# Causal attention on one core: the weighing of values moved from the pause between rounds into the round, and the diagonal's maxima split and taken one round later

## The chip, the cores and the metric

The kernel runs on one core of a Trainium2 chip. The metric is the device time of one execution in microseconds (us). A core has five engines that matter here: PE (TensorE, matrix products, with PEld for its weight loads), DVE (VectorE), ACT (ScalarE), POOL (GpSimd) and SP (SyncE, which issues DMAs). Each engine [...]waits for the others by semaphores. Products land in PSUM, which has 8 banks of 512 fp32 columns by 128 partitions.

## The reference

Four sequences of 1024 tokens with 128 features pass four residual blocks: an attention with relative positions, a mixture-of-experts FFN, a causal attention with one shared key and value head, and the same FFN again. The change touches the third block alone:

```python
def _L0_attn_b_ref(x, Wq, bq, Wk, bk, Wv, bv, Wo, bo):
    NUM_HEADS = 16; HEAD_DIM = D_MODEL // NUM_HEADS          # 8
    q = (x @ Wq + bq).reshape(b, t, NUM_HEADS, HEAD_DIM)
    k = x @ Wk + bk                                         # one head for all
    v = x @ Wv + bv
    scores = einsum('bthd,bsd->bhts', q, k) / sqrt(HEAD_DIM)
    scores = scores * mask - 1e10 * (1 - mask)              # causal
    probs = softmax(scores, axis=-1)
    out = einsum('bhts,bsd->bthd', probs, v).reshape(b, t, 128)
    return out @ Wo + bo
x = x + _L0_attn_b_ref(_layernorm(x), ...)
```

## The kernel before

All four blocks are one program. The first attention takes the first 1600 us or so, the FFN f follows (overlapped with the preparation of the causal attention, `b_prep`, line 912), the causal attention runs from about 1800 to 2585 us, and the FFN g ends the program. All of it is written by hand in one order (`tc.manual_schedule()`, line 1165): what the Python calls emit first stands first in each engine's queue.

**The tiles.** A tile n is 128 queries (block i of sequence b). There are 32; `tiles` (line 949) orders them so that each sequence begins while the one before it ends. Heads lie as 4 row groups g (of 32 partitions, 8 of them used and a ninth for the maximum) by 4 positions k, so one product with K = 32 rows of the array serves one group.

**Scores** (`b_scores`, line 959) are computed twice. The first time, with the queries as weights, is only for the maxima: a step is one PSUM bank of `s_b`. The first four steps of a tile are the diagonal block; ACT copies them to `dg` (L980), POOL masks `dg` after the fourth (L988). Steps of the earlier keys are reduced by DVE to `m2` straight from PSUM (L982). In the tile's last step DVE reduces all of `dg` (L993), and a small reduce (L997) writes the negated maxima of all chunks into `mpad`. `found` then holds the tile.

**Queries** (`b_queries`, line 1003): PE turns `mpad` (`mt`, L1008), and DVE adds it to the queries (`qm`, L1010), so that the second product has the maximum subtracted already.

**Weights** (`b_weights`, line 1016): for each key block j, the diagonal first, four products `t_b` (L1027), one for each row group, with the keys as weights and 512 columns (4 positions x 128 queries). ACT exponentiates each into `pt` (L1030). A diagonal `pt` is masked by POOL (L1034). After the fourth group the block is appended to `waiting`.

**Weighing** (`b_weigh`, line 1041): four products `o_b` (L1048), all 128 rows by 32 columns of the array, accumulate one key block into a PSUM bank of a pool of two (`small`). After the tile's last block ACT copies the sum to `oT` (L1055), and a generator `b_out` (line 1058) is put on `going`. Its steps are: nothing, then `tp` (four transposes, L1065, with DVE's `oinv` and `on`), then `y` (one transpose, ACT copies `onT`), then `z` (one product, DVE adds to x). Each call advances it by one.

Every fp32 product appears as two records on PE. `s_b`, `t_b`, `mt`, `tp`, `y`, `z` and the preparation take their banks from one pool of six (`one`, line 733), in which a bank comes free when its reader has read it.

**The rounds** (`causal_attention`, line 1084). There are 576 `t_b` products, 8 to a round, so 72 rounds. Score steps are spread before them: the loop at L1088 finds how many must be done by each round (a tile's scores two rounds ahead of its weights), and CAP limits a round to 10. In round r the loop L1118 to L1122 emits, for q = 0 to 7, one or two score steps and one weight step. Behind the eight comes what I call the pause (L1127 to L1143): the weighing of all waiting blocks but the last two, so of the two blocks that the round before produced; `mt` and `qm` of tiles that were found one round ago (`lag`); one step of each output generator; steps of `b_prep` for the next sequence; and steps of the FFNs (`left_over`, `sending`).

Of the kernel before, what the change touches and what calls it, by code (L numbers as in the profile page):

```python
# [12 lines left out]
F32 = mybir.dt.float32  # L13
I32 = mybir.dt.int32
AF = mybir.ActivationFunctionType
ALU = mybir.AluOpType
AX = mybir.AxisListType

P = 128
# [11 lines left out]
NH = 16  # L31
HD = 8
# [32 lines left out]
def block_kernel(ctx: ExitStack, tc: tile.TileContext, a: dict, out: bass.AP):  # L65
    nc = tc.nc
# [682 lines left out]
    chunks = [(b, c, min(4, TILES - c)) for b in range(B) for c in range(0, TILES, 4)]  # L749
# [199 lines left out]
    tiles = sorted(((b, i) for b in range(B) for i in range(NB)), key=lambda t: (t[1] + 4 * t[0], t))  # L949


    ROUND = 8
    first_round, count = [], 0
    for b, i in tiles:
# [4 lines left out]
    def b_scores(n):  # L959


        b, i = tiles[n]
        qa, ka, _ = prepared[b]
        tok = slice(i * P, (i + 1) * P)
        m2 = fp.tile([P, NH, 3], F32, tag="m2", name=f"m2_{n}")
        dg = fp.tile([P, NH, P], F32, tag="wide", name=f"dg_{n}", bufs=6)
        chunks = [(i * P, P)] + [(c, min(512, i * P - c)) for c in range(0, i * P, 512)]
        steps = []
        for c, (k0, w) in enumerate(chunks):
            nh = min(4, 512 // w)  # L970
            steps += [(c, k0, w, k, nh, g) for k in range(0, 4, nh) for g in range(4)]
        for at, (c, k0, w, k, nh, g) in enumerate(steps):
            ps = one(f"s_b{n}_{at}")
            for q in range(nh):
                nc.tensor.matmul(  # L975
                    ps[:, q * w : (q + 1) * w], qa[rows[g], k + q, tok],
                    ka[rows[g], k0 : k0 + w], start=True, stop=True,
                )
            if c == 0:
                nc.scalar.copy(dg[:, 4 * g : 4 * (g + 1), :].rearrange("p k c -> p (k c)"), ps)  # L980
            else:
                nc.vector.tensor_reduce(  # L982
                    m2[:, 4 * g + k : 4 * g + k + nh, c],
                    ps[:, : nh * w].rearrange("p (k c) -> p k c", c=w), AX.X, ALU.max,
                )
            if at == 3:

                nc.gpsimd.affine_select(  # L988
                    out=dg, in_=dg, pattern=[[0, NH], [-1, P]], compare_op=ALU.is_ge,
                    fill=NEG, base=0, channel_multiplier=1,  # L990
                )
            if at == len(steps) - 1:
                nc.vector.tensor_reduce(m2[:, :, 0], dg, AX.X, ALU.max)  # L993
                mpad = mpads[n % 4]
                mview = mpad.rearrange("p k (g r) -> p g k r", g=4)[:, :, :, HD]
                mv4 = m2.rearrange("p (g k) c -> p g k c", g=4)
                nc.vector.tensor_reduce(  # L997
                    mview, mv4[:, :, :, : len(chunks)], AX.X, ALU.max, negate=True
                )
                found.append(n)  # L1000
            yield

    def b_queries(n):

        b, i = tiles[n]
        mt = one(f"mt_{n}")
        for k in range(4):
            nc.tensor.transpose(mt[:, k * P : (k + 1) * P], mpads[n % 4][:, k, :], ident)  # L1008
        qm = fp.tile([P, 4, P], F32, tag="qm", name=f"qm_{n}", bufs=4)
        nc.vector.tensor_tensor(  # L1010
            qm, prepared[b][0][:, :, i * P : (i + 1) * P],
            mt.rearrange("p (k c) -> p k c", k=4), ALU.add,
        )
        queries[n] = qm

    def b_weights(n):

# [23 lines left out]
    def b_weigh(n, j, pt):  # L1041
        b, i = tiles[n]
        va = prepared[b][2]
        if n not in sums:
            sums[n] = small(f"o_b{n}")
        op = sums[n]
        for g in range(4):
            nc.tensor.matmul(  # L1048
                op[g * 32 : (g + 1) * 32, :], va[:, j, :], pt[:, g, :],
                start=(j == i), stop=(i == 0 or j == i - 1),  # L1050
            )
        if i == 0 or j == i - 1:

            oT = fp.tile([P, 4, P], F32, tag="oT", name=f"oT_{n}", bufs=4)
            nc.scalar.copy(oT.rearrange("p k c -> p (k c)"), sums.pop(n))  # L1055
            going.append(b_out(n, oT))

    def b_out(n, oT):

        b, i = tiles[n]  # L1060
        x_t = xs[b][:, i, :]
        yield
        tp = one(f"tp_b{n}")
        for k in range(4):
            nc.tensor.transpose(tp[:, k * P : (k + 1) * P], oT[:, k, :], ident)  # L1065
        o4 = tp.rearrange("p (k g w) -> p g k w", k=4, g=4)
        oinv = fp.tile([P, 4, 4, 1], F32, tag="oinv", name=f"oinv_{n}")
        nc.vector.reciprocal(oinv, o4[:, :, :, HD : HD + 1])
        on = fp.tile([P, 4, 4, HD], F32, tag="on", name=f"on_{n}", bufs=4)
        nc.vector.tensor_tensor(  # L1070
            on, o4[:, :, :, :HD], oinv.to_broadcast([P, 4, 4, HD]), ALU.mult
        )
        yield
        yp = one(f"y_b{n}")
        nc.tensor.transpose(yp[:, :P], on.rearrange("p g k w -> p (g k w)"), ident)
        onT = fp.tile([P, P], F32, tag="onT", name=f"onT_{n}", bufs=4)
        nc.scalar.copy(onT, yp[:, :P])
        yield
        zp = one(f"z_b{n}")
        nc.tensor.matmul(zp[:, :D], onT, bwo, start=True, stop=True)  # L1080
        nc.vector.tensor_tensor(x_t, x_t, zp[:, :D], ALU.add)
        finished.append(n)

    def causal_attention(left):

        steps_of = [sum(4 * (4 // min(4, 512 // w)) for w in chunk_widths(i)) for b, i in tiles]
        must = []
        for r in range(-2, ROUNDS):  # L1088
            must.append(sum(x for x, f in zip(steps_of, first_round) if f <= r + 2))

        CAP = 10
        cum = list(must)
        for r in range(len(cum) - 2, -1, -1):
            cum[r] = max(cum[r], cum[r + 1] - CAP)
        scores = (None for n in range(len(tiles)) for _ in b_scores(n))
        weights = (None for n in range(len(tiles)) for _ in b_weights(n))

        start = {b: next(r for r, c in enumerate(cum) if c > sum(steps_of[: tiles.index((b, 0))]))
                 for b in range(2, B)}
        coming = {b: b_prep(b) for b in range(2, B)}  # L1100
        second = next(r for r, c in enumerate(cum) if c > sum(steps_of[: tiles.index((1, 0))]))
        taken = 0
        lag = []
        sending, sent, left_over = [], 0, list(left)
        for k, r in enumerate(range(-2, ROUNDS + 4)):
            for b in coming:
                if k == start[b]:
                    for _ in coming[b]:
                        pass
            if k == second:  # L1110
                while 1 not in prepared:
                    left_over = [g for g in left_over if next(g, 0) is None]
            upto = cum[min(k, len(cum) - 1)]
            mine = upto - taken
            taken = upto
            if 0 <= r < ROUNDS:
                given = 0
                for q in range(ROUND):  # L1118
                    while given * ROUND < mine * (q + 1):
                        next(scores)  # L1120
                        given += 1
                    next(weights)  # L1122
            else:
                for _ in range(mine):
                    next(scores)

            now, waiting[:] = waiting[:-2] if r < ROUNDS - 1 else waiting[:], waiting[-2:] if r < ROUNDS - 1 else []  # L1127
            for w in now:
                b_weigh(*w)
            ready, lag = lag, list(found)  # L1130
            found.clear()
            for n in ready:
                b_queries(n)
            going[:] = [g for g in going if next(g, going) is not going]
            for b in coming:
                for _ in range({9: 2, 8: 1, 7: 4}.get(start[b] - k, int(0 < start[b] - k < 7))):
                    next(coming[b], None)
            left_over = [g for g in left_over if next(g, 0) is None]

            if sent < B - 1 and tiles.index((sent, NB - 1)) in finished:  # L1140
                sending.append(sends("g", sent, (1, 3)))
                sent += 1
            sending = [g for g in sending if next(g, 0) is None]  # L1143
        return sending, list(range(sent, B))

    def chunk_widths(i):
# [10 lines left out]
    mpads = []  # L1157
# [3 lines left out]
        mpads.append(mpad)  # L1161

    prepared, queries, sums, found, waiting, going, finished = {}, {}, {}, [], [], [], []

    with tc.manual_schedule():
        left = ffn("f", {
# [74 lines left out]
```

## Time and profile before

| what | us |
|---|---|
| median of three runs (lowest to highest) | 2808.8 (2784.7 to 2812.8) |
| the profiled execution, its own time | 2796.1 |
| its span, first to last instruction | 2794.4 |
| DVE, ACT busy from 1832.2 to 2580.0 (747.8 us) | 431.8, 445.8 |
| t_b products L1027: records, one | 1152, 0.59 at least |
| s_b products L975: records, one | 2304, 0.27 to 0.59 by width |
| o_b products L1048: records, one | 1152, 0.59 |
| exp L1030, one | 0.60 |
| score maxima L982, one | 0.54 to 0.70 |
| POOL's masks L988 and L1034, one | 2.01 |
| qm L1010, one | 0.69 |

How to read it: a record's busy time on PE runs from its start to a modelled end, and records overlap, so that a busy PE can still be made faster if more of its products run at once. PEld is the weight load of a product; its idle time and the releaser of it show what PE's queue waits for. A releaser called "issue" means that the profile shows nothing that was waited for. In the view of waits a line gives the waiting engine and line, the releaser, and then the total in us, the number of times and the longest. The granted clock is TensorE's, 1.00 being full speed.

### The profile page before, as it was taken

The numbers are of one execution on the slowest core, as the hardware profiler recorded it, in microseconds if no ns is written. First come the engines' busy times: TensorE is split into PE (matmuls) and PEld (weight loads), VectorE is DVE, ScalarE is ACT, GpSimd is POOL, SyncE is SP. The second block draws the span as 40 slices with busy tenths as digits, with TensorE's granted clock in tenths as the row PEclk, the third lists the DMA queues.
The fourth block names the chain that finished last, engine by engine and source line by source line (L and its number), as shares of the span: only waits on it lengthen the run. The fifth ranks groups of instructions, "written<-read, shape, count | busy, mean of one in ns | idle before, by whom it ended". The sixth has DMA issues, their size and how long they took to land.

```text
span 2794.4 us, 47349 instructions
## 1 busy us (share of the span) xinstructions
PE 2700.6 (97%) x18928; PEld 1665.0 (60%) x18928; DVE 1406.5 (50%) x3278; ACT 1333.8 (48%) x2478; POOL 540.3 (19%) x693
## 2 busy tenths in 40 slices
PE   6999999999999999999999999999999999999895
PEld 3465666666565656565666676666456456554663
DVE  2335454545545454535454545466546456574444
ACT  2444454443444443534444344555656656556442
POOL 3111000000200001200002006542212215122365
PEclk9999999999999999999999999889989889999897
DMA  8577565664757565657566413200000001000243
GB/s 217 186 245 227 185 199 194 215 200 161 233 169 233 174 204 170 228 173 233 197 213 217 152 49 108 71 14 3 1 1 1 1 1 31 1 7 11 63 119 99
DMA packets 148491, 363.59 MB, mean 130 GB/s; under 512 B 16160, under 2 KB 71872, under 8 KB 147952
## 3 DMA queue, kind: packets, MB, share of 16 engines
q1 hardware_dynamic: 130128, 316.78, 34.9%
q0 software_dynamic: 15552, 40.97, 5.6%
q10 hardware_dynamic: 2592, 2.82, 0.4%
q8 instruction: 150, 2.46, 0.4%
q14 instruction: 69, 0.57, 0.1%
HBM read 176.69 MB, written 183.76 MB: 129 GB/s over the span
## 4 chain that ended last, share of the span: by engine, by line
PE 92%; DVE 2%; issue 2%; DMA 1%; POOL 1%; ACT 1%; another core or an unknown queue 0%; POOLq 0%; ACTq 0%; DVEq 0%
PE op L616 16%; PE rp L555 16%; PE sp L583 15%; PE s_b L975 10%; PE t_b L1027 9%; PE o_b L1048 5%; PE h_f L790 3%; PE h_g L790 3%; PE rt L559 2%; PE yp L635 2%; PE kp L537 2%; PE yp_f L819 1%; PE yp_g L819 1%; PE qk_b L929 1%; PE rkps L502 1%
## 5 line engine op out<-in xcount | busy, mean ns | idle before, releaser
L588 DVE CUSTOM_DVE_ANT_0 s<-sp,s 128x1024 f32<-128x1024 f32 x256 | 313.1, 1223 | 373.8 <-PE sp L583 368.5
L593 ACT ACTIVATE s<-s,nmax 128x1024 f32<-128x1024 f32 x256 | 294.0, 1149 | 416.4 <-DVE nmax L588 409.4
L583 PE MATMUL sp<-kT,xT 128*128 128x512 f32 x1024 | 484.3, 596 | 1.6 <-ACT kT L542 1.6
L616 PE MATMUL op<-at,xrep 32*128 32x256 f32 (+1 forms) x8448 | 454.8, 370 | 3.4 <-DVE nmax L588 3.1
L616 PEld LDWEIGHTS op<-at,xrep 32*128 32x128 f32 x8448 | 422.9, 186 | 47.0 <-issue 23.5
L1027 PE MATMUL t_b<-qm,ka_b 32*128 32x512 f32 x1152 | 439.5, 650 | 3.8 <-DVE m L982 1.7
L975 PE MATMUL s_b<-ka_b,qa_b 32*128 32x128 f32 (+3 forms) x2304 | 424.6, 418 | 1.2 <-DVE m L982 0.9
L1030 ACT ACTIVATE pt_b<-t_b 128x512 f32<-128x512 f32 x576 | 329.1, 610 | 167.7 <-PE t_b L1027 131.7
L982 DVE TENSOR_REDUCE m<-s_b 128x1 f32<-128x512 f32 (+3 forms) x480 | 287.5, 649 | 113.6 <-PE s_b L975 85.2
L602 DVE STREAM_TRANSPOSE at<-s 128x1024 f32<-128x1024 f32 x256 | 315.8, 1238 | 0.2 <-ACT s L593 0.2
L975 PEld LDWEIGHTS s_b<-ka_b,qa_b 32*128 32x128 f32 x2304 | 265.0, 197 | 71.2 <-issue 21.1
L555 PE MATMUL rp<-relk,xT 128*128 128x512 f32 x640 | 303.0, 596 | 0.0
L560 ACT COPY xr<-rp 128x1024 f32<-128x1024 f32 x256 | 256.4, 1002 | 68.4 <-issue 36.5
L583 PEld LDWEIGHTS sp<-kT,xT 128*128 128x128 f32 x1024 | 175.1, 191 | 127.2 <-issue 123.3
L628 DVE COPY oT<-op 128x256 f32<-128x256 f32 (+1 forms) x66 | 24.4, 411 | 397.7 <-PE op L616 397.7
L1027 PEld LDWEIGHTS t_b<-qm,ka_b 32*128 32x128 f32 x1152 | 158.3, 188 | 88.3 <-DVE m L982 42.1
L555 PEld LDWEIGHTS rp<-relk,xT 128*128 128x128 f32 x640 | 116.4, 190 | 127.1 <-issue 124.7
L626 ACT COPY oT<-op 128x256 f32<-128x256 f32 (+1 forms) x66 | 20.9, 369 | 350.9 <-PE op L616 350.9
L170 POOL COPY beats<-beats 1x1 f32<-1x1 f32 x240 | 43.2, 180 | 618.4 <-DVE beats L167 615.8
L1048 PE MATMUL o_b<-pt_b,va_b 128*32 128x512 f32 x1152 | 148.7, 637 | 0.0
L555 PE MATMUL rp<-w,xT 128*128 128x512 f32 x256 | 121.2, 596 | 1.4 <-ACT xr L560 1.4
L988 POOL TENSOR_SCALAR_AFFINE_SELECT dg<-dg 128x2048 f32<-128x2048 f32 x32 | 64.2, 2007 | 219.5 <-ACT dg L980 219.5
(276 smaller groups left out, 3085.0 us busy)
## 6 DMA issues: line engine op xcount, KB each, us to landing
skew<-xr SPq DMA_DIRECT2D x256, 576.0 KB
s<-skew SPq DMA_DIRECT2D x256, 512.0 KB
ring<-sorted SPq DMA_DIRECT2D x40, 256.0 KB
xrep<-stored POOLq DMA_DIRECT2D x16, 512.0 KB
sorted<-ident POOLq DMA_DIRECT2D x4, 1472.0 KB
res_f<-y_f SPq DMA_DIRECT2D x20, 256.0 KB
res_g<-y_g SPq DMA_DIRECT2D x20, 256.0 KB
w<-in_w POOLq DMA_DIRECT2D x16, 256.0 KB
```

Of the source, the lines that this page charges most:

```text
L555: nc.tensor.matmul(rp[:, c, :], lhsT, rk[:, base + c * 512 : base + (c + 1) * 512], start=True, stop=True)
L560: nc.scalar.copy(xr[:, :L], rp.rearrange("p a c -> p (a c)"))
L583: nc.tensor.matmul(sp[:, c, :], xTs[b][:, i * P : (i + 1) * P], kT[:, c * 512 : (c + 1) * 512], start=True, stop=True,)
L588: nc.vector.tensor_tensor_reduce(out=s, in0=sp.rearrange("p a c -> p (a c)"), in1=s, scale=-1.0, scalar=BIG, op0=ALU.add, op1=ALU.min, acc ...
L593: nc.scalar.activation(s, s, AF.Exp, bias=nmax, scale=-1.0, accum_out=total)
L602: nc.vector.transpose(sums[m][:, i, :], s)
L616: nc.tensor.matmul(ops[g // 2][:, g % 2, :n], xrep[r, j, :], at[r, tiles, j * 32 : (j + 1) * 32], start=(j == 0), stop=(j == 31),)
L975: nc.tensor.matmul(ps[:, q * w : (q + 1) * w], qa[rows[g], k + q, tok], ka[rows[g], k0 : k0 + w], start=True, stop=True,)
L982: nc.vector.tensor_reduce(m2[:, 4 * g + k : 4 * g + k + nh, c], ps[:, : nh * w].rearrange("p (k c) -> p k c", c=w), AX.X, ALU.max,)
L1027: nc.tensor.matmul(ps, ka[rows[g], j * P : (j + 1) * P], qm[rows[g], :], start=True, stop=True)
L1030: nc.scalar.activation(pt[:, g, :], ps, AF.Exp, scale=HD ** -0.5)
L1048: nc.tensor.matmul(op[g * 32 : (g + 1) * 32, :], va[:, j, :], pt[:, g, :], start=(j == i), stop=(i == 0 or j == i - 1),)
```

## The change

1. The weighing of the two blocks of the round before is emitted within the round, one block behind the weight step q = 3 and one behind q = 6 (`WEIGHED`), and no longer in the pause. In the last round the pause weighs what is left.
2. The diagonal's reduce is taken out of the last score step into a generator `b_diagonal`. It does the first eight heads behind q = 1 of the next round, and the other eight and the small reduce into `mpad` behind q = 4. `m2` has four buffers for that.
3. `lag` is gone: a tile that is found in a round has its queries made in that round's pause. With 2 that is the same pause as before.
4. The output steps (`going`) are advanced behind q = 3, ahead of the weighing there, and not in the pause; the generator's empty first step is gone.

```diff
@@ b_scores
-        m2 = fp.tile([P, NH, 3], F32, tag="m2", name=f"m2_{n}")
+        m2 = fp.tile([P, NH, 3], F32, tag="m2", name=f"m2_{n}", bufs=4)
...
             if at == len(steps) - 1:
-                nc.vector.tensor_reduce(m2[:, :, 0], dg, AX.X, ALU.max)
-                mpad = mpads[n % 4]
...
-                found.append(n)
+                diagonals.append(b_diagonal(n, dg, m2, len(chunks)))
             yield
+
+    def b_diagonal(n, dg, m2, count):
+        for half in range(2):
+            heads = slice(half * NH // 2, (half + 1) * NH // 2)
+            nc.vector.tensor_reduce(m2[:, heads, 0], dg[:, heads, :], AX.X, ALU.max)
+            if half == 0:
+                yield
...
+        nc.vector.tensor_reduce(mview, mv4[:, :, :, :count], AX.X, ALU.max, negate=True)
+        found.append(n)
@@ b_out
         x_t = xs[b][:, i, :]
-        yield
         tp = one(f"tp_b{n}")
@@ causal_attention
         CAP = 10
+        WEIGHED = (3, 6)
...
+            due, diagonals[:] = list(diagonals), []
+            behind, waiting[:] = list(waiting), []
             if 0 <= r < ROUNDS:
...
                     next(weights)
+                    if q in (1, 4):
+                        for d in due:
+                            next(d, None)
+                    if q == 3:
+                        going[:] = [g for g in going if next(g, going) is not going]
+                    if q in WEIGHED and behind:
+                        b_weigh(*behind.pop(0))
             else:
                 for _ in range(mine):
                     next(scores)
-
-            now, waiting[:] = waiting[:-2] if r < ROUNDS - 1 else waiting[:], waiting[-2:] if r < ROUNDS - 1 else []
-            for w in now:
+                for d in due:
+                    for _ in d:
+                        pass
+                going[:] = [g for g in going if next(g, going) is not going]
+            if r == ROUNDS - 1:
+                behind, waiting[:] = list(waiting), []
+            for w in behind:
                 b_weigh(*w)
-            ready, lag = lag, list(found)
+            ready = list(found)
             found.clear()
             for n in ready:
                 b_queries(n)
-            going[:] = [g for g in going if next(g, going) is not going]
```

## The prediction

> **What bounds the kernel now.** I read the page from the top: busy shares, slices, chain, then only the stretch that the change touches.
>
> ```profile
> PE 2700.6 (97%) x18928; PEld 1665.0 (60%) x18928; DVE 1406.5 (50%) x3278; ACT 1333.8 (48%) x2478; POOL 540.3 (19%) x693
> ...
> PEclk9999999999999999999999999889989889999897
> ...
> PE 92%; DVE 2%; issue 2%; DMA 1%; POOL 1%; ACT 1%; another core or an unknown queue 0%; POOLq 0%; ACTq 0%; DVEq 0%
> PE op L616 16%; PE rp L555 16%; PE sp L583 15%; PE s_b L975 10%; PE t_b L1027 9%; PE o_b L1048 5%; PE h_f L790 3%; PE h_g L790 3%; PE rt L559 2%; PE yp L635 2%; PE kp L537 2%; PE yp_f L819 1%; PE yp_g L819 1%; PE qk_b L929 1%; PE rkps L502 1%
> ```
>
> The chain lies on PE; the lines that move (s_b, t_b, o_b) hold a quarter of it. The first score product of a weighted round starts at 1832.2 us and the last round's t_b ends at about 2578: 72 rounds in 748 us, 10.4 us each. Next I cut three rounds into body (first t_b to the first o_b), weighing, and rest of the pause, in the view by windows:
>
> ```profile
> 2130.05:2137.82 7.77, 7.77 (x37) 3.79 (x37) 7.27 (x20) 4.48 (x8) 1.65 (x1) 1.00 0.00 0
> 2137.82:2139.67 1.85, 1.85 (x17) 0.41 (x16) 0.00 (x0) 0.60 (x1) 0.00 (x0) 1.00 0.03 9
> 2139.67:2142.10 2.43, 2.43 (x25) 2.00 (x23) 1.66 (x6) 0.00 (x0) 0.00 (x0) 1.00 0.00 0
> 2142.10:2147.81 5.71, 5.71 (x48) 4.38 (x43) 5.51 (x10) 3.88 (x7) 0.00 (x0) 1.00 0.00 1
> 2147.81:2149.66 1.85, 1.85 (x18) 0.41 (x16) 1.83 (x3) 0.69 (x2) 0.00 (x0) 1.00 0.00 0
> ```
>
> Columns: window, length, then PE, PEld, DVE, ACT, POOL busy. PE is busy in all of them. DVE fills these two bodies to 94% and 97%, and stands still in the first weighing (0.00 of 1.85). That idleness is what the change would use. But it is worth time only where PE would go faster for it. So: what does PE wait for within a round, and what does an interruption of its products cost?
>
> ```profile
> PEld o_b L1048 <- issue: 99.8, 211, 1.5
> PEld t_b L1027 <- DVE m L982: 42.1, 90, 1.5
> ...
> PEld s_b L975 <- DVE m L982: 19.0, 62, 1.4
> ...
> PEld t_b L1027 <- ACT pt_b L1030: 12.8, 34, 1.5
> ...
> PEld s_b L975 <- ACT pt_b L1030: 7.4, 28, 0.5
> ...
> PEld t_b L1027 <- ACT dg L980: 2.6, 11, 0.4
> ...
> PEld s_b L975 <- ACT dg L980: 1.6, 8, 0.2
> ```
>
> These are the weight loads of the whole attention stretch: total us, times, longest. The six lines on DVE and ACT are waits for a free PSUM bank, together 85.5 us. The o_b line is no wait for data: the load of the weighing can't be drawn ahead of products of another form.
>
> ```profile
> 2136.44 0.59 PE L975 MATMUL s_b<-ka_b,qa_b 32*128 32x512 f32 x1
> 2136.87 1.02 PE L1027 MATMUL t_b<-qm,ka_b 32*128 32x512 f32 x2
> 2137.82 1.92 PE L1048 MATMUL o_b<-pt_b,va_b 128*32 128x512 f32 x16
> 2139.68 0.66 PE L1008 MATMUL mt<-ident,mpad 128*128 128x128 f32 x4
> ```
>
> The order of time on PE at the end of that body. The 16 o_b records start in four bursts 0.43 us apart (1.92 us minus one record of 0.62 is three steps), so 512 columns stream in 0.43 us, one tile's weighing takes 0.86 and two take 1.72. The second t_b pass starts at 2137.30 in the trace; 2137.73 is its end of streaming, o_b starts 0.09 later. The last burst starts at 2139.13, ends at 2139.56, and mt starts 0.12 later.
>
> **The change part by part.**
>
> **1. The weighing itself** costs the same wherever it stands: 72 x 1.72 = 124 us of PE. Moved: 0.
>
> **2. Breaks.** s_b and t_b run on different groups of 32 rows at once: their streaming in the stretch sums to some 1000 us (485 + 514, columns at 512 per 0.43 us and the granted clock), in bodies of 463 us. o_b takes all rows, so it can start only when the last t_b is through, and nothing overlaps across it. For each round I took the end of streaming of the fourth and the seventh t_b (second pass start + 0.43) and subtracted the start of the next product behind it: that overlap is lost. Mean over 72 rounds: 0.38 us (q=3) and 0.59 us (q=6), 0.97 a round, x 71 = 69 us. Two transitions of 0.09 + 0.12, x 2 x 71 = 30 us. The pause gives back: in 45 of 71 pauses whole-array work stays (mt, preparation, the next FFN's routing), so only 0.12 goes; in the other 26 only o_b and the three output steps stood there, both transitions go (0.21) and the last t_b overlaps the next round's first product (0.49, the mean of the two above). 45 x 0.12 + 26 x 0.70 = 24 us. Gross **+75 us**, for 116 breaks more (2 x 71 + 45 against 71).
> Here the Trainium skill speaks against the change: TensorEngine Tiling, Key Properties, says that a change of tiling mode drains the engine. It gives no time. By the rule with only an empty pipe (a record's 0.59 less 0.43 of streaming is 0.16 us, once out and once in) the 116 breaks would be 116 x 0.32 = 37 us; the rows give 75, because besides the drain the concurrency of row groups goes. I take 75; the ends are 37 and 99, the latter if today's pauses give nothing back.
>
> **3. What the breaks give back.** While PE weighs, DVE and ACT empty the six banks, so the next six products meet no bank wait. Today only the first six of about 18 products of a round do; then products 10 to 15 and 17 to 18 do too: 8 of the 12 that can wait now. 85.5 x 2/3 = 57 us; since part of such a wait lies beside the other row group's streaming (PE has hardly a gap), I take half of 85.5: **-43 us**, ends 0 and -85.
>
> **4. The diagonal's maxima.** One DVE reduce of 2.28 us becomes two.
>
> ```profile
> L993 DVE TENSOR_REDUCE m<-dg x32: 2266/2278/2289, 1811.3 to 2546.5; 128x16 f32<-128x2048 f32 x32
> ...
>   POOL dg L988: 27.2, 4
> ...
>   PEld s_b L975: 0.3, 1
> ```
>
> A half has 1024 elements: about 1.17 us (half, plus a small fixed part, an estimate). The 27 us in which DVE stood before four of them, waiting for POOL's mask, are gone after the change, but only one weight load ever waited on them (0.3 us): 0. Behind the block of 2.28 us, s_b reduces came 1.6 to 2.9 us late in some six rounds; about 1 us each is saved: -6. The halves now stand ahead of s_b reduces at q=1 and q=4, where DVE is 94 to 97% full in many rounds; each delays a bank by 1.2 us: +2. Queries (mt) come out of the same pause as before, as the extra round of lag is dropped for them. Net **-4 us**, ends -15 and +20.
>
> **5. The output steps** (tp, y, z; 8 + 1 + 2 short products a tile, with two DVE operations, one ACT copy, one DVE add) go to q=3, in the break that exists there: their PE time is the same. They take three more slots of the six-bank ring in the body, and behind oinv on DVE wait the next s_b reduces. They also no longer cover the 0.9 us from mt's end (2140.17 in that pause) to qm's (2141.06), which the first t_b of a new tile needs (PE t_b <- DVE qm is 0.8 us in all now): 30 x 0.2 us, and 2 for the ring: **+8 us**, ends 0 and +30. No DMA is moved; SP's and POOL's orders keep their places, and the weighing of a masked tile at q=3 comes at least 3 us after POOL's mask of 2.0 us.
>
> **6. The clock.** Over 1832 to 2580 the granted clock is 0.96, in the worst 100 us (1800 to 1900) 0.82: half rate for 2 x 0.04 x 748 = 60 us. The skill's TensorE: Matmul & The Clock Gate, Part 1, ties half rate to an idle window of about 3.4 us; PE's longest gap in this stretch is 1.5 us, so by the rule there would be none, before or after, and the change would win nothing. The row disagrees: half rate comes here without such a gap. If the denser or the broken-up body changes that, the sum moves by up to 60/2 = 30 us either way. I take 0.
>
> **Sum:** 75 - 43 - 4 + 8 = **+36 us**, about 0.5 us a round. The profiled execution took 2796.1 us (span 2794.4 and 1.7 around it); the median of the runs shown is 2808.8, of 2784.7 to 2812.8, a spread of 1%, which is about what a measurement of this kernel can tell from no change. I add to the middle of profile and median, 2802: **2838 us**.
>
> **The rivals.**
> *The bodies are bound by the drains (faster), 15%.* The skill's TensorEngine Tiling, PSUM Bottleneck, says that with a faster tiled TensorE the PSUM copy may become the limit, and DVE at 97% of a body agrees. Then a break costs PE only time in which it would have waited: half of the lost overlap (34) + 30 - 24 = 40, less all 85 of the waits, less 4 and plus 8: -41 at most, about -25 likely: 2777 us. Against it: at the end of the fourth and seventh t_b most rounds show ACT only that one exp behind (0.69 us), so results don't queue. It decides from 75 us of waits recovered.
> *It cancels, 35%.* Recovered 60 and output steps free: +11, 2813 us. Also the case if the clock gains some 20 us.
> *DVE becomes the bound, 12%.* In the some 40 rounds with ten s_b reduces DVE has about 0.6 us of backlog at a break; until the next score lands pass 0.09 + 0.86 + 0.12 + 1.1 (two passes) = 2.2 us, so DVE idles 1.6 us twice, 3.2 against 1.8 to 2.8 in today's pause with the qm and maxima in it. +1.2 x 40 = 48 on top of my sum: 2886 us.
> *The forecast, 38%*, +20 to +60: 2822 to 2862.
>
> **How the numbers follow.** Faster by over 1%: the first rival, 0.15. Within 1%: the second, with the low edge of the forecast, 0.37. Slower: the rest, 0.48. Range: leaving out half of the first rival and most of the third, 2780 to 2876.
>
> **What would show it.** Right: o_b records in two groups of 8 a round; the stretch of 748 us grows to some 784; weight loads of s_b and t_b waiting on DVE and ACT fall from 85 to about 45 us, while o_b's line on "issue" grows beyond 100; 64 reduces of dg at about 1.2 us. Wrong: bodies that grow by less than 1.7 us although they hold the o_b (the first rival), DVE waiting on PE s_b for more than now in total (the third), or a clock well off 0.96, which would make the sum right or wrong by accident.

## The result, and the profile after

The changed kernel takes 2890.2 us in the median of its four runs (2885.1 to 2905.3), the kernel before 2796.8 us in four (2784.7 to 2812.8; three of them are those of the table above). The ratio is **1.035 [1.029, 1.041]**: slower, by more than twice what was forecast, and above the upper end of the range (2876). The profiled execution took 2888.2 us (span 2886.5), against 2796.1 (span 2794.4): 92 us more between the spans.

From the page of the changed kernel, the busy shares, the granted clock in 40 slices, and the chain:

```profile
PE 2792.0 (97%) x18928; PEld 1645.1 (57%) x18928; DVE 1417.7 (49%) x3310; ACT 1334.8 (46%) x2478; POOL 538.5 (19%) x693
...
PEclk9999999999999999999999999698999999989997
...
PE op L616 16%; PE rp L555 15%; PE sp L583 15%; PE s_b L976 10%; PE t_b L1036 9%; PE o_b L1057 6%; PE h_f L790 3%; PE h_g L790 2%; PE yp L635 2%; PE rt L559 2%; PE kp L537 2%; PE yp_f L819 1%; PE qk_b L929 1%; PE yp_g L819 1%; DMA skew<-xr 1%
```

The chain still lies on PE and the number of its records is the same. The row of the clock is too coarse to judge by: it has a 6 in the 26th slice (1804 to 1876 us), where the attention begins, but fewer 8s behind it than before. The attention from its first t_b to its last shows more, in the view by windows (window, length, then busy us and instructions of PE, PEld, DVE, ACT and POOL, then the granted clock, the DMA share and GB/s), for the kernel before:

```profile
1832.20:2577.30 745.10, 737.08 (x4941) 408.91 (x4939) 431.78 (x886) 443.44 (x837) 188.80 (x163) 0.96 0.02 7
```

and for the changed kernel:

```profile
1834.00:2680.20 846.20, 835.82 (x4959) 392.39 (x4958) 444.32 (x925) 445.49 (x840) 186.66 (x160) 0.92 0.02 6
```

The reader is to see three things: 101 us more, although DVE and ACT are busy for nearly as long as before; PE "busy" through all of it; and a clock of 0.92 where the sum had assumed 0.96. (What lies behind the last t_b is 11 us shorter than before, 206.3 for 217.1, which is why the stretch grows by more than the span.)

The weight loads of this stretch and what they waited for, in the view of waits (us, times, longest), in the changed kernel:

```profile
PEld o_b L1057 <- issue: 71.5, 124, 1.5
PEld s_b L976 <- issue: 51.2, 109, 1.7
PEld t_b L1036 <- DVE m L983: 46.7, 74, 1.6
PEld s_b L976 <- DVE m L983: 43.9, 78, 1.5
PEld t_b L1036 <- issue: 28.8, 93, 1.7
PEld t_b L1036 <- ACT pt_b L1039: 24.3, 29, 1.5
PEld s_b L976 <- ACT pt_b L1039: 18.0, 25, 0.9
...
PEld s_b L976 <- ACT dg L981: 12.0, 14, 1.0
```

The waits for a bank, which I had expected to fall from 85 to about 45 us, rose to 146 (46.7 + 43.9 + 24.3 + 18.0 + 12.0, and 1.1 of the sixth line, which is not shown). The o_b line on "issue" fell from 99.8 to 71.5, where the prediction had it grow. The prediction read that line wrongly. In the trace of before, 71 loads of o_b stand idle behind a product of another form, 55 us together; another 146, 49 us, wait between the bursts of one weighing. In the changed kernel it is 124 loads and 72 us behind another form, and under 1 us between bursts: the part that belongs to the breaks did grow. Behind a break s_b and t_b stand in the same way: their lines on "issue" grew from 42 us together (20.8 and 21.5) to 80.

The waits of DVE and ACT for products, before:

```profile
DVE m L982 <- PE s_b L975: 81.3, 58, 8.5
...
ACT pt_b L1030 <- PE t_b L1027: 131.7, 159, 4.7
...
ACT pt_b L1030 <- PE s_b L975: 31.9, 57, 4.2
```

After:

```profile
DVE m L983 <- PE s_b L976: 211.5, 110, 11.2
...
ACT pt_b L1039 <- PE t_b L1036: 247.3, 213, 5.1
```

In these lines DVE stands still for PE 130 us longer, ACT 116 us longer. That speaks against either engine as the limit, but doesn't show the cause: both have about the same work as before, so a stretch that is 101 us longer leaves DVE 89 us more idle and ACT 99, whatever lengthened it.

Last, the place of the prediction's worked example. The round that answers to the one with a body of 7.77 us begins with the t_b at 2171.58 in the changed kernel. In the view by windows: its first products (with the last two of the round before, as no work stands in that pause now), the output steps, the first weighing, products, the second weighing, and the products behind it:

```profile
2171.55:2176.71 5.16, 5.16 (x26) 2.17 (x22) 3.96 (x14) 2.97 (x5) 1.82 (x2) 1.00 0.00 0
2176.71:2177.74 1.03, 1.03 (x10) 0.86 (x9) 1.03 (x3) 0.60 (x1) 0.00 (x0) 1.00 0.00 0
2177.74:2178.73 0.99, 0.99 (x9) 0.15 (x8) 0.96 (x4) 0.00 (x0) 0.00 (x0) 1.00 0.03 8
2178.73:2181.69 2.96, 2.96 (x19) 1.19 (x15) 2.28 (x6) 0.88 (x2) 0.00 (x0) 1.00 0.00 0
2181.69:2182.68 0.99, 0.99 (x9) 0.15 (x8) 0.96 (x3) 0.70 (x2) 0.00 (x0) 1.00 0.08 17
2182.68:2184.59 1.91, 1.91 (x8) 0.66 (x4) 1.73 (x3) 0.00 (x0) 0.00 (x0) 1.00 0.00 0
```

and in the order of time on PE:

```profile
2171.58 0.69 PE L1036 MATMUL t_b<-qm,ka_b 32*128 32x512 f32 x1
...
2181.69 1.07 PE L1057 MATMUL o_b<-pt_b,va_b 128*32 128x512 f32 x8
2182.68 1.12 PE L976 MATMUL s_b<-ka_b,qa_b 32*128 32x512 f32 x2
2183.65 1.02 PE L1036 MATMUL t_b<-qm,ka_b 32*128 32x512 f32 x2
2184.59 0.66 PE L1016 MATMUL mt<-ident,mpad 128*128 128x128 f32 x4
```

From the first t_b to mt it was 9.62 us (2130.05 to 2139.68, body and weighing) and is 13.01 (2171.58 to 2184.59). The output steps are 1.03 of that; they stood behind mt before. Each weighing fills 0.99 us, as expected: two passes of 0.43 and the two transitions. The rest is the products of s_b and t_b themselves: 7.77 us in one piece, and now 5.13 + 2.96 + 1.91 = 10.00 in three (beside the first run the last two products of the round before). The last of the three is the plainest. One s_b and one t_b stand alone between a break and the pause's mt, and by the kernel's order use the same row group: they run one after the other, each with two passes of 0.43, and nothing runs beside them. Behind mt 0.87 us are won back (1.55 instead of 2.42 to the next round's first t_b), so that the round is 2.52 us longer (14.56 for 12.04). Only one round lost more: the 51 rounds that lie at the full clock in both traces are 0.90 us longer in mean.

### The profile page after: what moved, and what is told of

It is laid out like the page before. It is cut to its first block, busy times and chain, and to the rows that moved or that the text cites. A ratio compares the mean times of both kernels' runs of the same rounds, so it can differ in the third digit from the quotient of the medians.

```text
span 2886.5 us, 47381 instructions
## 1 busy us (share of the span) xinstructions
PE 2792.0 (97%) x18928; PEld 1645.1 (57%) x18928; DVE 1417.7 (49%) x3310; ACT 1334.8 (46%) x2478; POOL 538.5 (19%) x693
## 4 chain that ended last, share of the span: by engine, by line
PE 91%; DVE 3%; DMA 2%; issue 2%; POOL 1%; ACT 1%; SPq 0%; POOLq 0%; DVEq 0%; ACTq 0%
PE op L616 16%; PE rp L555 15%; PE sp L583 15%; PE s_b L976 10%; PE t_b L1036 9%; PE o_b L1057 6%; PE h_f L790 3%; PE h_g L790 2%; PE yp L635 2%; PE rt L559 2%; PE kp L537 2%; PE yp_f L819 1%; PE qk_b L929 1%; PE yp_g L819 1%; DMA skew<-xr 1%
## 5 line engine op out<-in xcount | busy, mean ns | idle before, releaser
L1039 ACT ACTIVATE pt_b<-t_b 128x512 f32<-128x512 f32 x576 | 328.8, 601 | 320.4 <-PE t_b L1036 247.3
L1036 PE MATMUL t_b<-qm,ka_b 32*128 32x512 f32 x1152 | 461.6, 667 | 6.6 <-DVE m L983 3.7
L616 PEld LDWEIGHTS op<-at,xrep 32*128 32x128 f32 x8448 | 423.1, 186 | 46.7 <-issue 23.5
L976 PEld LDWEIGHTS s_b<-ka_b,qa_b 32*128 32x128 f32 x2304 | 248.6, 207 | 170.7 <-issue 53.1
L1036 PEld LDWEIGHTS t_b<-qm,ka_b 32*128 32x128 f32 x1152 | 152.7, 195 | 112.4 <-DVE m L983 46.7
L1057 PE MATMUL o_b<-pt_b,va_b 128*32 128x512 f32 x1152 | 170.2, 667 | 0.0
```

The lines of the kernel that those rows point to most:

```text
L616: nc.tensor.matmul(ops[g // 2][:, g % 2, :n], xrep[r, j, :], at[r, tiles, j * 32 : (j + 1) * 32], start=(j == 0), stop=(j == 31),)
L976: nc.tensor.matmul(ps[:, q * w : (q + 1) * w], qa[rows[g], k + q, tok], ka[rows[g], k0 : k0 + w], start=True, stop=True,)
L1036: nc.tensor.matmul(ps, ka[rows[g], j * P : (j + 1) * P], qm[rows[g], :], start=True, stop=True)
L1039: nc.scalar.activation(pt[:, g, :], ps, AF.Exp, scale=HD ** -0.5)
L1057: nc.tensor.matmul(op[g * 32 : (g + 1) * 32, :], va[:, j, :], pt[:, g, :], start=(j == i), stop=(i == 0 or j == i - 1),)
```

## The experiments

All were run on the kernel before or the changed one with a short edit. Products that are added write to a bank that nobody reads. Each ratio is to runs of the kernel before on the same chip. Where a granted clock differs, I also give a **clock-free** cost. It comes from 27 runs of the kernel before, four sets of six or seven, each set on one chip: their clocks lie between 0.959 and 0.979, and within a set a run is longer by 0.42 us for each us that the clock stood at half rate (2 x (1 - clock) x span). Clock-free cost = difference of the medians after 0.42 of each kernel's half-rate time is taken off. The runs scatter about that line by 2 us; for kernels with a clock under 0.959 it is drawn on beyond what was measured. For the changed kernel, +61, only one run of the kernel before has its clock on record (2796.1 us at 0.974). Theories in the expectations: A, the breaks between row groups and the whole array; B, the split maxima; C, the output steps in the ring; D, that the clock follows what PE does.

**1. The weighing alone.** Everything else stays as before.

```diff
+            behind, waiting[:] = list(waiting), []
             ...
                     next(weights)
+                    if q in (3, 6) and behind:
+                        b_weigh(*behind.pop(0))
...
-            now, waiting[:] = ...
-            for w in now:
+            if r == ROUNDS - 1:
+                behind, waiting[:] = list(waiting), []
+            for w in behind:
                 b_weigh(*w)
```

> The kernel before with one part of the change alone: the weighing stands behind q = 3 and q = 6 of the round; the diagonal's maxima and the output steps stay as they were. Theory A, breaks: each place at which PE turns from row-group products to the weighing and back costs lost overlap and two transitions, and nothing comes back; 142 breaks more, gross 69 + 30 - 9 = 90 us, and more of the stretch at half clock: 2870 to 2900 us. Theory B, the split maxima: this part alone costs 20 us or less, below 2820. Theory C, the output steps in the ring: about 2830.

Measured: 2881.1 us, 1.034 [1.028, 1.041], the whole loss; clock-free +77. Its stretch in the view by windows (columns as above):

```profile
1827.20:2669.50 842.30, 828.23 (x4958) 387.03 (x4955) 436.18 (x886) 446.71 (x840) 188.61 (x163) 0.94 0.02 6
```

and the waits of DVE and ACT in it:

```profile
DVE m L982 <- PE s_b L975: 214.5, 119, 7.2
...
ACT pt_b L1030 <- PE t_b L1027: 262.2, 220, 5.0
```

Both are close to those of the changed kernel (211.5 and 247.3). So the place of o_b is enough for the loss.

**2. The maxima alone**, in halves behind q = 1 and q = 4 of the next round.

```diff
-                nc.vector.tensor_reduce(m2[:, :, 0], dg, AX.X, ALU.max)
...
+                diagonals.append(b_diagonal(n, dg, m2, len(chunks)))
...
+                    if q in (1, 4):
+                        for d in due:
+                            next(d, None)
...
-            ready, lag = lag, list(found)
+            ready = list(found)
```

> The kernel before with the diagonal's maxima in halves one round later, alone. Theory A, breaks: within 10 us of before, as no break is added. Theory B, split maxima: the halves stand ahead of score maxima on DVE while it is over 90 per cent full, 1.2 us each; the rounds that hold them carry the loss (1.8 to 2.1 us there, 0.2 in rounds of the same sort without them): plus 40 to 60 us, 2837 to 2857.

Measured: 2831.9 us, 1.016 [1.010, 1.022]; clock-free +15. Here a theory that looks at waits alone would go wrong. In the 55 rounds that lie at the full clock in both traces the mean difference is 0.10 us: 41 agree to 0.01 us, eight are 0.74 to 1.09 us longer, and six differ by less, most of them shorter. That is 7 us over 71 rounds; where the other 8 are I can't say. More than half of the loss is the clock:

```profile
1833.60:2617.80 784.20, 771.42 (x4941) 421.26 (x4939) 432.70 (x914) 442.93 (x837) 186.29 (x159) 0.92 0.02 6
```

The granted clock fell from 0.96 to 0.92, though PE has the same records in nearly the same order.

**3. The output steps alone**, behind q = 3.

```diff
@@ b_out
-        yield
...
                     next(weights)
+                    if q == 3:
+                        going[:] = [g for g in going if next(g, going) is not going]
...
-            going[:] = [g for g in going if next(g, going) is not going]
```

> The kernel before with the output steps behind q = 3, alone. Theory A, breaks: some 64 rounds get one break more, of 0.38 of lost overlap and 0.21 of transitions, and their pause loses next to nothing: plus 38 us, 2835. Theory C, the ring and DVE's queue: plus 60 or more. Theory B: within 10 us of before.

Measured: 2838.5 us, 1.019 [1.012, 1.025]; clock-free +29. By themselves they make breaks of their own: PE changes its form (row groups, column groups or the whole array) 319 times in the stretch instead of 214, some 52 breaks more, and at the 0.38 + 0.21 of the expectation these are 31 us. In the changed kernel they share the weighing's break and so cost nothing more: the clock-free cost of both together is 71 (experiment 5), of the weighing alone 77.

**4. Both weighings in one break**, the changed kernel with two o_b groups behind q = 3.

```diff
-                    if q in WEIGHED and behind:
+                    while q == 3 and behind:
                         b_weigh(*behind.pop(0))
```

> The changed kernel with both weighings behind q = 3, so one break in the round and not two. Theory A, breaks: the break behind q = 6 cost 0.59 + 0.21 in each of 71 rounds, 57 us, which go, with a part of the half clock: 2820 to 2840. Theory B: as the changed kernel within 20 us, as the maxima stay where they are. Theory C: as the changed kernel.

Measured: 2851.8 us, 1.022 [1.016, 1.029]; 38 us less than the changed kernel, and clock-free +38 against +61. Theory A is right in sign, but the second break is cheaper here than the 57 us that it named. PE changes its form 446 times in the changed kernel's stretch, 304 times in this one and 214 times before; the 142 changes that were saved, 71 breaks, are worth 23 us clock-free, 0.32 a break. (The rounds at the full clock say nearly the same: 0.51 us longer than before in mean, for 0.90 in the changed kernel.) Why half of their price came back isn't shown; a longer first break may let DVE and ACT run dry for longer.

**5. The changed kernel without the late maxima**: weighing and output steps as changed, the diagonal's reduce and `lag` as before.

```diff
-                diagonals.append(b_diagonal(n, dg, m2, len(chunks)))
+                nc.vector.tensor_reduce(m2[:, :, 0], dg, AX.X, ALU.max)
...
```

> The changed kernel with the diagonal's maxima put back as they were, in one piece in the tile's last step; the weighing and the output steps stay inside the round. Theory A, breaks: the output steps share the break behind q = 3, so nothing is added to the kernel with the weighing alone (2881), and pauses that are left empty give some back: 2865 to 2885. Theory B, the maxima carry a loss of their own, which the kernel with the maxima alone shows in eight rounds (0.7 to 1.1 us each) at an unchanged clock: 10 to 16 us below the changed kernel, 2874 to 2880. Theory D, the clock is the main thing: the time follows the granted clock, by 0.42 us for each us at half rate.

Measured: 2926.6 us against 2819.5 for the kernel before on that chip, 1.037 [1.029, 1.045]; clock-free +71. Rival B falls: without the split maxima the kernel isn't faster, and its rounds at the full clock are about as long as the changed kernel's: 0.83 us longer than before in mean, for 0.90 (the round shown above is 2.52 us longer than before in both).

**6 and 7. Breaks without work.** To the kernel before, one product of the whole array with 8 columns is added behind q = 3, or behind q = 3 and q = 6. No other engine gets anything from it. It takes a bank of the ring of six, though, and so can itself wait for one.

```diff
                     next(weights)
+                    if q in (3, 6):
+                        ps = one(f"e_{r}_{q}")
+                        nc.tensor.matmul(ps[:, :8], ident, bwq[:, :8], start=True, stop=True)
```

> The kernel before with an added product in each round behind q = 3: whole array, 8 columns, into a bank that nobody reads. It measures a break by itself; nothing else is moved. Theory A: 0.38 of lost overlap + 0.21 for two transitions + about 0.15 for the product's two loads, x 72 = 53 us at the same clock: 2850 or somewhat more. If breaks give the drains time that comes back later (what I predicted): 53 - 20 = 33. If the cost of the change is in the moved work and not in the breaks: under 15.

> As the one before, with the same empty product behind q = 3 and q = 6. Theory A: (0.97 + 0.42 + 0.30) x 72 = 122 us at the same clock: 2920. If what a break gives the drains comes back: about 80. If breaks cost nothing: 2810 or below.

Measured: one break 2918.1 us, 1.032 [1.026, 1.038], clock-free +47 (expected 53), which is 0.65 us a break. Two breaks 3023.4 us, 1.070 [1.065, 1.075], clock-free +122, as worked out from the trace of before. In the stretch, all instructions and then the added tile alone:

```profile
1835.40:2812.60 977.20, 969.93 (x5223) 489.22 (x5223) 435.18 (x888) 447.38 (x838) 188.54 (x163) 0.83 0.02 5
...
1835.40:2812.60 977.20, 62.24 (x288) 49.01 (x288) 0.83 0.02 5
```

The added product's waits in the view of waits:

```profile
PEld e L1125 <- DVE m L982: 73.9, 85, 1.5
...
PEld e L1125 <- ACT pt_b L1030: 25.8, 29, 1.5
```

This is the plainest view of the mechanism: 144 products that stream 8 columns each lengthen the stretch by 232 us. About half of that is the lost overlap and the transitions that part 2 of the prediction counts, and the added products' own loads. The other half is the clock, 0.83: half rate for 328 of 977 us. Yet it isn't a break alone: in most rounds the added product waits for a bank, and by these two runs that can't be told from the overlap. The weighing of experiment 1 takes no bank of the ring, and loses as much as the changed kernel.

**8 and 9. Does the clock follow the use of the array?** First the breaks of 7 again, with 512 columns in place of 8 (more work, and more of the array used); then a full product behind the second score step of every tile in the kernel before.

```diff
-                        nc.tensor.matmul(ps[:, :8], ident, bwq[:, :8], start=True, stop=True)
+                        nc.tensor.matmul(ps, ident, bwq, start=True, stop=True)
```

> The kernel with two empty breaks a round, with the empty products (8 columns) made full ones (128 x 128 x 512, two passes of 0.43 us): the same breaks in the same places, 144 x 0.8 = 115 us more of PE work that fills the array. If half rate follows from too little of the array streaming in a window of 3.41 us (under 0.375), most of the half rate goes: from a granted clock of 0.937 to 0.97 or more over the whole, some 200 us less at half rate, 84 us back at 0.42: about 1.08 times before, only 10 to 40 us over the kernel with empty breaks. If half rate follows from breaks, from waits or from the time of day: the clock stays near 0.94 and the time is 1.07 times before + 115 us, 1.11 times before.

```diff
@@ b_scores, after the step's products
+            if at == 1:
+                fill = one(f"fill_{n}")
+                nc.tensor.matmul(fill, ident, bwq, start=True, stop=True)
```

> The kernel before with an added product of 128 x 128 x 512 behind the second of each tile's four diagonal score steps (32 in all), into a bank that nobody reads: it fills the array where the score products of 128 columns leave three quarters of its rows idle. Theory D, the clock goes to half in a window of 3.41 us that follows one in which the products that stream cover less than 0.375 of the array: such windows get fewer, the granted clock over the whole rises from 0.969 to 0.975 or more, and of the 32 x (0.86 + 0.6) = 47 us of added time some 15 to 25 come back: 2820 to 2835. If half rate has another cause: the clock stays at 0.969 or falls, and the time is 2845 or more.

Measured: the filled breaks take 3049.8 us, 1.080 [1.074, 1.087], that is 1% more than the empty ones (by the two ratios; the runs were on different chips). In the stretch:

```profile
1835.40:2829.00 993.60, 985.63 (x5249) 446.02 (x5251) 434.12 (x888) 451.03 (x842) 188.96 (x163) 0.93 0.02 5
...
1835.40:2829.00 993.60, 178.83 (x288) 46.01 (x288) 0.93 0.02 5
```

The clock came back from 0.83 to 0.93 (143 us at half rate instead of 328), and that paid for most of 90 us of added streaming: clock-free it costs 212, the empty one 122. This is what D expects and a clock that is lowered by more work would not give. The second kernel missed: 2862.2 us, 1.016 [1.010, 1.022], clock-free +40 (expected 47), with clocks of 0.962 to 0.969 where D expected 0.975 or more. 32 full products were too few or not where the clock fell; it doesn't speak against D, and doesn't support it.

**10 and 11. Neighbours on the same row group.** The round shown above had raised the question of whether the order of row groups matters. Here the order of the four t_b of a key block is chosen so that each lies two groups away from the last score step's, in the kernel before, and then in the changed one.

```diff
+            free = [0, 1, 2, 3]
...
-                g = (gi + 2) % 4
+                g = next(x for d in (2, 3, 0, 1) if (x := (scored[-1] + d) % 4) in free)
+                free.remove(g)
@@ b_scores
+            scored.append(g)
```

> The kernel before with another order of the four row groups of a key block's weight products: each takes, of the groups still open, the one two away from the score step emitted last (then three, then none). Nothing is added or moved otherwise. If bodies are bound by how many row groups run at once, fewer neighbours fall on the same rows, products overlap more, and the kernel is faster by 10 to 40 us at the same clock, with more than that if windows of low use get fewer. If bodies are bound by the drains (DVE and ACT): within 5 us of before.

> The changed kernel with the other order of row groups that made the kernel before 0.983 of its time. Theory A, breaks: what is lost is overlap between row groups, so the break's price stays or grows as there is more overlap to lose; the change costs again 60 to 75 us at the same clock and some 25 by the clock: 1.015 to 1.03 times before, well above 0.983. Rival: with products that flow better PE runs ahead and the drains become the bound, so that weighing within the round pays at last: 0.983 or below.

Measured: on the kernel before **2772.3 us against 2814.7, 0.983 [0.978, 0.988]**, faster than both kernels; clock-free -30. On the changed kernel 2865.3 against 2823.7, 1.016 [1.009, 1.024], clock-free +32. The change thus costs the same, clock-free +62 us, on either order (+61 on the order as given): the order is not what makes it slow, it is a gain by itself. The faster kernel's stretch:

```profile
1837.00:2553.30 716.30, 706.00 (x4941) 396.79 (x4939) 432.46 (x886) 442.17 (x837) 188.66 (x163) 0.96 0.02 7
```

with the waits of ACT in it:

```profile
ACT pt_b L1035 <- PE s_b L976: 73.5, 82, 3.9
ACT pt_b L1035 <- PE t_b L1032: 61.3, 110, 3.6
```

ACT's line on t_b is halved from 131.7 us, but its line on s_b grew from 31.9; together they fall by 29 us, no more than the stretch is shorter. What shows the cause is the rounds. In the order as given, 23 of the 71 rounds have, by the kernel's source, every t_b beside score steps of its own group. Of these 14 lie at the full clock in both traces, the one shown above among them, and all are shorter, by 1.14 to 3.46 us, 2.06 in mean. The other 41 change by -0.19 to +1.32, +0.44 in mean.

## Why the prediction was wrong

The direction and its cause were right: the change was slower, by breaks in PE's products. The size was wrong by 56 us between the spans (92 against 36). Two terms of the sum hold it: the relief that the breaks were to give back (part 3, 43 booked, 17 came), and the clock (part 6, 0 booked, 31 came).

**Part 2, the breaks (75): right in sum.** The 116 breaks are there: PE changes its form 446 times instead of 214, 232 = 2 x 116 more. The lost overlap can be checked round by round, since part 2 took it from each round of the trace of before. Rounds at the full clock in both traces, the mean lengthening from each round's own overlaps and transitions beside what was measured (the worked-out columns are estimates, the sum of part 2 for just those rounds; for the empty breaks with 0.30 for their loads):

| rounds | weighing alone: worked out | measured | two empty breaks: worked out | measured |
|---|---|---|---|---|
| all | 1.22 | 0.98 | 1.74 | 1.53 |
| ten score maxima on DVE | 1.24 | 1.21 | 1.75 | 1.75 |
| ACT also copies the diagonal | 1.38 | 0.87 | 1.83 | 1.15 |

The lower price, 37 us for drains of an empty pipe alone, by which I had read the Trainium skill's rule (TensorEngine Tiling, Key Properties), doesn't hold: one empty break cost 0.65 us where two transitions are 0.21. The rest is the added product's own loads (0.15 by the expectation's estimate) and the overlap of the row groups on either side of it, with what the product waits for its bank. One thing does not fit: by part 2 the break behind q = 6 costs 57 us, and without it 23 came back (experiment 4).

**Part 3, what the breaks give back (43): failed.** The sum said that DVE and ACT empty the six banks during a break, so that the next six products meet no wait, and took half of 85 us. The table shows what came: 1.22 - 0.98 = 0.24 us a round, 17 us over 71 rounds, and next to nothing in rounds with ten score maxima, the most frequent kind. More came back only where ACT also copies the diagonal (1.38 to 0.87, 1.83 to 1.15); a backlog of ACT's that a break works off would give that. The error was to read the six waits as a debt that is carried from product to product, which an idle moment of PE's pays off. They rose to 146 us instead. My reading is that DVE works at the same pace as PE in these rounds: a break empties its queue, then it waits for PE, and when it gets products again it is as late for the banks as ever. That the relief is missing is measured; this reason for it is argued from the waits, as no run here has a faster DVE.

**Part 4, the maxima (-4): small as forecast, not understood.** 64 reduces of 1.209 us, for an estimate of 1.17:

```profile
L1001 DVE TENSOR_REDUCE m<-dg x64: 1192/1209/1215, 1823.6 to 2650.8; 128x8 f32<-128x1024 f32 x64
```

With the weighing inside no cost of theirs shows: the kernel without them is clock-free at 71, the changed one at 61, but the two were run on different chips, on which even the kernel before differs by nearly 20 us. Alone they cost 15, within the ends given (-15 and +20) and of the other sign.

**Part 5, the output steps (+8): agrees.** Alone they cost 29, about what the 52 breaks of experiment 3 come to. With the weighing they fill a break that exists, and take the 26 pauses' transitions away (15 us of part 2): 77 for the weighing alone, 71 with them, where the sum has 77 - 15 + 8.

**Part 6, the clock (0): failed.** Half rate over the span went from 145 us (2 x 0.026 x 2794) to 219 (2 x 0.038 x 2887), 74 more, which at 0.42 is **31 us**: the end that I had given. Alone it lies within the range; with the 26 us of part 3 the sum leaves it. I had written that a denser or more broken-up body could move it, and took the middle because I had no rule. The rule of an idle window of about 3.4 us (the Trainium skill, TensorE: Matmul & The Clock Gate, Part 1), which I had set aside because the row spoke against it, doesn't explain it here either: by the view of waits the longest idle time in the changed stretch is 1.1 us before a product and 1.9 before a weight load (1.4 and 1.7 in the kernel before, for which the prediction gave 1.5). (The 0.82 of 1800 to 1900 us that part 6 read as the worst of the stretch lies mostly ahead of it; within it the worst 100 us of the kernel before are 0.87, from 2200 to 2300.)

With the two terms as measured: 75 - 17 - 4 + 8 + 31 = 93 us, for 92 between the spans.

**The rivals.** *Drains-bound* and *it cancels* are out with part 3. *DVE becomes the bound* named 2886 us, and its sign, DVE's growing wait for s_b, appeared, as it would in any longer stretch. And its mechanism isn't what the runs show: it adds a cost of DVE on top of the breaks, and rounds with ten score maxima cost what the breaks cost alone (1.21 for 1.24). It was right that those rounds get no relief. The agreement in time is by accident: 26 us of relief that didn't come and 31 of the clock.

**What stays open.** The clock's rule below is a fit to records, supported by one pair of kernels. Which rounds fall to half rate varies from run to run of the same kernel (clocks of 0.959 to 0.979), so the 31 us are those of these runs. The reason why the relief of part 3 stayed out is argued, not tested, and why the second break alone is so cheap isn't known. And the steps from 77 to 71 to 61 us lie close to what chips differ by.

## What to carry to other kernels

Where products use parts of the array side by side, an interruption by another form costs the overlap on both sides of it: read it from the trace, product by product, before moving work "into the gaps", and keep the foreign work in one place. Don't book relief from a break by the sum of waits: ask in which rounds the reading engine has a backlog, and where it would run dry instead. The order of products that share row groups is worth a look first, since here it gave 1.7% for a reordering that adds no instruction.

## What was not expected of the hardware

**The granted clock follows how much of the array is used, not whether PE idles.** In the attention stretches of 13 kernels I cut the time into steps of 3.413 us, the grid on which the granted clock changes. For each window I summed, over all products, streaming time (0.43 us for 512 columns) x rows x columns of the array in use, as a share of the whole array for the whole window. Of 2628 windows at the full clock 200 are followed by half rate. A share below 0.375 tells them from the others with 17 exceptions, which all lie between 0.357 and 0.411. A window at half rate returns to full if it did the work of a share of 0.75 at its own rate, and else stays: 545 windows, 26 exceptions. A product with 32 rows and 128 columns uses a quarter of the array, so two at a time give 0.5, and a round in which they stand alone, or wait at a break, falls below. PE is "busy" there all the while. In the kernel before, 48 of the 61 us at half rate lie in the 23 rounds whose neighbours share a row group. Windows at the full clock, placed at every phase of the grid, lie below 0.375 in 5.0% of the cases before, 6.9% in the changed kernel, 14.6% with two empty breaks and 2.6% with the filled ones; their clocks in the stretch are 0.96, 0.92, 0.83 and 0.93. The last shows that this share alone does not order the kernels: once at half rate, the way back matters too.

**Half rate costs less than it seems**: 0.42 us for each us at half rate, not 0.5, by the 27 runs. And chips differ: the kernel before, clock-free, takes 2722 us in one of the four sets and 2740 to 2742 in the others.
